# A decoder layer on one core: the opening of the kernel written out in source order

## The chip, the core and the metric

The kernel runs on one core of a Trainium2 chip. A core has five engines that run at the same time and wait for one another through semaphores: PE (TensorE, the matrix engine; its weight loads are listed as PEld), DVE (VectorE), ACT (ScalarE), POOL (GpSimd) and SP (SyncE, which here only issues DMA transfers). Each engine works through its own list of instructions in order; an instruction that waits holds up all behind it on that engine. Data lie in main memory (HBM), in the core's working memory (SBUF, 128 partitions) and in the matrix engine's result memory (PSUM, eight banks, written by PE).

The metric is the device time of one execution in microseconds (us); smaller is better. A profile is one execution recorded instruction by instruction. Its *span* runs from the first to the last instruction; the execution's own time is a little longer. The profile also records the clock that PE was granted: 1.00 is full speed.

## The reference, cut to what matters

A batch of 16 sequences of 256 tokens with 512 features goes through one decoder layer: causal self-attention, a long convolution against a context, and a feed-forward step, each followed by a residual sum and a layer norm. All projections use weights rounded to three values (-1, 0, 1) with one scale per weight matrix, and activations rounded to 8 bits with one scale per token.

```python
def _bitlinear(x, w):
    sw = 1.0 / clip(mean(abs(w)), 1e-05, None)          # one number per weight matrix
    wq = clip(round(w * sw), -1.0, 1.0) / sw
    sx = 127.0 / clip(max(abs(x), axis=-1), 1e-05, None)  # one number per token
    xq = clip(round(x * sx), -128.0, 127.0) / sx
    return einsum('bse,oe->bso', xq, wq)

q, k, v = _bitlinear(x, w_q), _bitlinear(x, w_k), _bitlinear(x, w_v)
attn = softmax(where(causal, q k^T / sqrt(32), -1e30))
x = layernorm(x + _bitlinear(attn v, w_o))
x = layernorm(x + long_convolution(ctx, ctx, x, ssm_kernel, D))
x = layernorm(x + feed_forward(x, gamma, W))           # W rounded to three values as well
```

So there are five weight matrices of 512 x 512 (`w_q`, `w_k`, `w_v`, `w_o`, `w_f`). Each needs, before it can be used: the mean of its absolute values (a sum along each partition, then a sum over the partitions), the reciprocal of that, a scaling and rounding (adding the large number MAGIC rounds a float to an integer), a clamp to -1..1, and a store as bf16.

## The kernel before, in words

The kernel has three parts, one after the other.

**The opening (lines 37 to 126).** All inputs of the opening are loaded: `first` (batch 0 of x, 0.5 MB) and the five raw weights (1 MB each) over the two DMA queues of SP and ACT, then the convolution's taps (`rows`, 80 KB). GpSimd builds constants (`ident`, `mask_f`, `pick_f`, `col`). Then a loop over the five weights (L99 to L121) does for each: the absolute sum (L104 on DVE for the first three, L107 on ACT for the last two), the sum over partitions as a product with a matrix of ones (`total`, L109), the scale and its inverses (L111 to L116), the two rounding passes (L119 and L120, on DVE for weights 0 and 2, on POOL for weights 1, 3 and 4), and the bf16 store on ACT (L121). `rows` gets its diagonal term and is written to main memory as `taps` (L124, L125). The order of these instructions on each engine is not the source's: this part stands outside the block whose order is written by hand, and a planner has placed it.

**Layer 1, the attention (lines 160 to 481).** It works on one batch at a time, in a software pipeline: `step(b)` holds, in four groups g = 0..3, stages of several batches. For batch b + 1 it does `scan` (the scores once, only for the row maxima), for b `weigh` (scores again, exponential) and `values`, for b + 2 `turn_in`, `project_qk` and `project_v` (the three projections), for b + 3 `fetch_x` and the rounding of x (`fetch_scales`, `fetch_scaled`, `fetch_rounded`), for b - 1 the output projection, and for b - 2 the norm and `keep`, which stores the result, transposed, in `x1t`. `x1t` is one large SBUF tile that layer 2 reads. `step(-2)`, with the first batch's projections, is still placed by the planner; from `step(-1)` on the order on PE, ACT, DVE and POOL is the source's (`tc.manual_schedule`, L479). The DMA queues of SP are not in that list.

Scores of `scan` and `weigh` share one four-bank PSUM tile `s`: `scan` of one group cannot start before the reader of the previous scores is done. The small results (`acc`, `tp`, `row`, `total` in the changed kernel) rotate through three banks under the tag `misc`.

**Layer 2, convolution and feed-forward (lines 484 to 714).** It loops over 32 heads. For each head SP loads `c` (two transfers, L512 and L513) and `w` (L516, from `taps`); POOL multiplies pairs (`kv`, L521), PE does the convolution as matrix products (`y`, L546), and so on. Its SBUF tiles take the addresses that layer 1's pools gave back, and wait for the last users of those addresses. Which tiles meet which addresses follows from the order in which the pools are opened: layer 1's pool `xp` (x as loaded: `xt`, `xr`) is opened inside layer 1 and given back with it.

## Time and profile before

| what | value |
|---|---|
| median of 3 runs | 982.52 us (981.02 to 983.88) |
| the profiled execution's own time | 980.88 us |
| its span | 979.0 us |
| mean granted PE clock | 0.978 |
| busy share of the span | PE 89%, DVE 75%, POOL 50%, ACT 42% |
| weights landed (w_q, w_k, w_v, w_o, w_f) | 9.9, 13.1, 15.3, 18.5, 21.2 us |
| first product with a rounded weight (`acc`, L220) | 39.42 us |
| first scores (`scan`, L259) | 46.16 us |
| first product of layer 2 (`y`, L546) | 515.01 us |

A line of the timeline reads: start, duration, engine, line, operation, result <- operands, shapes, count; in brackets how long the engine was idle before it and what ended that. A line of windows reads: the stretch, then for each engine the busy time and the number of instructions, the granted clock, the DMA engines' busy share and the rate in GB/s. PE is busy nearly all the time, except in the first 46 us, around 60 us, around the border of the two layers near 500 us, and at the very end.

### The profile page before, as it was taken

The numbers are of one execution on the slowest core, as the hardware profiler recorded it, in microseconds if no ns is written. First come the engines' busy times: TensorE is split into PE (matmuls) and PEld (weight loads), VectorE is DVE, ScalarE is ACT, GpSimd is POOL, SyncE is SP. The second block draws the span as 40 slices with busy tenths as digits, with TensorE's granted clock in tenths as the row PEclk, the third lists the DMA queues.
The fourth block names the chain that finished last, engine by engine and source line by source line (L and its number), as shares of the span: only waits on it lengthen the run. The fifth ranks groups of instructions, "written<-read, shape, count | busy, mean of one in ns | idle before, by whom it ended". The sixth has DMA issues, their size and how long they took to land.

```text
span 979.0 us, 21212 instructions
## 1 busy us (share of the span) xinstructions
PE 867.2 (89%) x8349; PEld 626.0 (64%) x8426; DVE 734.5 (75%) x1947; ACT 415.7 (42%) x651; POOL 488.4 (50%) x569
## 2 busy tenths in 40 slices
PE   1488999999999999998758999999999999999992
PEld 1255666666666666665526777777777777777771
DVE  6465777777777777776444898888988898889885
ACT  2624565665656666665541232223322332223222
POOL 4413233222323323222228778777787778777850
PEclk9999999999999999999978999999999999999996
DMA  9000110011111110000022222122212222222100
GB/s 322 28 22 24 45 44 24 24 44 45 45 45 45 45 45 2 24 23 23 24 68 67 65 76 65 50 76 76 71 43 76 76 73 54 64 76 75 33 12 33
DMA packets 54739, 53.18 MB, mean 54 GB/s; under 512 B 19120, under 2 KB 35504, under 8 KB 54640
## 3 DMA queue, kind: packets, MB, share of 16 engines
q1 hardware_dynamic: 52816, 48.33, 16.7%
q10 hardware_dynamic: 1824, 3.49, 1.0%
q8 instruction: 67, 1.10, 0.4%
q14 instruction: 32, 0.26, 0.1%
HBM read 43.34 MB, written 8.47 MB: 53 GB/s over the span
## 4 chain that ended last, share of the span: by engine, by line
PE 53%; DVE 31%; ACT 6%; issue 6%; DMA 2%; POOL 2%; SPq 0%; ACTq 0%; DVEq 0%; POOLq 0%
PE y L546 8%; PE acc L220 6%; PE s L292 6%; PE pv L324 5%; PE s L259 4%; DVE st L582 4%; PE sums L331 4%; DVE turn L567 3%; PE acc_o L387 3%; PE acc_f L641 3%; PE tp L148 3%; PE acc_v L232 3%; DVE full L601 2%; PE s L252 2%; DVE r L643 2%
## 5 line engine op out<-in xcount | busy, mean ns | idle before, releaser
L546 PE MATMUL y<-kv,w 128*128 128x288 f32 x1280 | 335.2, 409 | 4.4 <-DMA c<-in_ctx_t 2.9
L546 PEld LDWEIGHTS y<-kv,w 128*128 128x128 f32 x1280 | 235.3, 192 | 60.5 <-POOL kv L521 5.6
L308 POOL TENSOR_SCALAR_AFFINE_SELECT p<-p 128x512 f32<-128x512 f32 x128 | 78.5, 638 | 256.9 <-ACT p L304 256.9
L673 POOL TENSOR_TENSOR own<-own,turn 128x512 f32<-128x512 f32 x128 | 162.9, 1273 | 78.6 <-DVE turn L567 60.7
L521 POOL TENSOR_TENSOR kv<-c 128x512 f32<-128x512 f32 (+1 forms) x192 | 182.2, 965 | 34.7 <-PE y L546 29.7
L264 DVE TENSOR_REDUCE nmax<-s 128x4 f32<-128x512 f32 (+1 forms) x128 | 116.6, 954 | 42.6 <-PE s L259 41.3
L304 ACT ACTIVATE p<-s 128x1536 f32<-128x1536 f32 x64 | 93.1, 1454 | 88.1 <-PE s L299 88.1
L590 ACT ACTIVATE root<-quarter 128x2 f32<-128x2 f32 x64 | 13.0, 203 | 210.2 <-DVE quarter L588 210.2
L575 PE MATMUL tok<-ident,own 128*128 128x128 f32 x640 | 91.0, 273 | 0.0
L575 PEld LDWEIGHTS tok<-ident,own 128*128 128x128 f32 x640 | 75.5, 141 | 16.2
L554 DVE SCALAR_TENSOR_TENSOR own<-y,q 128x128 f32<-128x128 f32 x128 | 36.0, 281 | 53.0 <-PE y L546 52.9
L220 PE MATMUL acc<-xit,w 128*128 128x256 bf16 x512 | 67.9, 278 | 5.8 <-ACT xit L149 5.8
L557 DVE TENSOR_TENSOR own<-y,q 128x384 f32<-128x384 f32 x128 | 69.7, 544 | 0.0
L567 DVE TENSOR_TENSOR turn<-y,q 128x384 f32<-128x384 f32 x128 | 69.6, 543 | 0.0
L292 PE MATMUL s<-qt,kt 32*128 32x256 f32 (+1 forms) x1024 | 60.4, 350 | 2.6 <-DVE nmax L264 2.5
L220 PEld LDWEIGHTS <-w 128*128 128x128 bf16 x512 | 46.2, 99 | 23.3 <-issue 13.4
L259 PE MATMUL s<-kt,qt 32*128 32x128 f32 (+1 forms) x1024 | 60.7, 352 | 0.0
L324 PE MATMUL pv<-p,va 128*32 128x256 f32 (+1 forms) x1024 | 55.9, 334 | 4.7 <-POOL p L308 3.3
L292 PEld LDWEIGHTS s<-qt,kt 32*128 32x128 f32 x1024 | 47.0, 186 | 17.1 <-issue 14.6
L331 PE MATMUL sums<-p,col 128*32 128x256 f32 (+1 forms) x1024 | 54.4, 329 | 0.0
L224 DVE SCALAR_TENSOR_TENSOR qt<-acc,q_scale,inv_row 128x512 f32<-128x512 f32 x32 | 24.0, 750 | 39.5 <-PE acc L220 39.4
L388 DVE SCALAR_TENSOR_TENSOR r<-acc_o,o_mul,xr 128x512 f32<-128x512 f32 x32 | 24.0, 750 | 38.0 <-PE acc_o L387 36.3
(125 smaller groups left out, 1355.5 us busy)
## 6 DMA issues: line engine op xcount, KB each, us to landing
xr<-in_x SPq DMA_DIRECT2D x16, 512.0 KB, 3.4
c<-in_ctx_t SPq DMA_DIRECT2D x32, 256.0 KB, 3.3
w<-taps SPq DMA_DIRECT2D x32, 256.0 KB, 3.6
out_y<-res SPq DMA_DIRECT2D x32, 256.0 KB, 2.3
xt<-in_x SPq DMA_DIRECT2D x15, 512.0 KB, 3.5
c<-in_ctx_t SPq DMA_DIRECT2D x32, 128.0 KB, 3.2
raw<-in_w_q ACTq DMA_DIRECT2D x1, 1024.0 KB, 9.1
raw<-in_w_k SPq DMA_DIRECT2D x1, 1024.0 KB, 11.8
```

Source lines behind the costliest of these rows:

```text
L220: nc.tensor.matmul(acc[:, j, :], w[:, c, o * P : (o + 1) * P], m.xit[:, c].rearrange("p t k -> p (t k)"), start=(c == 0), stop=(c == NB - 1),)
L259: nc.tensor.matmul(s[:, r, lo:hi], m.qt[rows, g, q0 : q0 + P], m.kt[rows, g, 0:nk], start=False, stop=True, skip_group_check=True,)
L264: nc.vector.tensor_reduce(view(m.nmax, t * NH + g, [[NB, 4]]), s[:, :, cols], AX.X, ALU.max, negate=True)
L292: nc.tensor.matmul(s[:, r, lo:hi], m.kt[rows, g, k0 : k0 + P], m.qt[rows, g, q0:S], start=(lo == 0), stop=False, skip_group_check=True,)
L304: nc.scalar.activation(p, s[:, :, 0 : 3 * P], AF.Exp)
L324: nc.tensor.matmul(acc[rows, q0:S], m.va[:, j, 4 * g + r, :], p[:, r, src], start=(j == 0), stop=(j == 1), skip_group_check=True, tile_pos ...
L331: nc.tensor.matmul(m.sums[rows, q0:S], col[:, g, :], p[:, r, src], start=(g == 0 and j == 0), stop=(g == NB - 1 and j == 1), skip_group_ch ...
L521: nc.gpsimd.tensor_tensor(kv[:, :, at : at + n * B].rearrange("p c (i b) -> p c i b", b=B), c[:, :, i : i + n, :], c[:, :, i + d : i + d + ...
L546: nc.tensor.matmul(y[:, Y0 + k * HALF : Y0 + (k + 1) * HALF], lhs, kv[:, mb, k * HALF : (k + 1) * HALF], start=(mb == 0), stop=(mb == lb),)
L567: nc.vector.tensor_tensor(view(t, B, [[P + B, 3], [1, P]]), view(y, Y0 + AT + P, [[P, 3], [1, P]]), view(q, base, [[0, 3], [1, P]]), ALU.mult,
L575: nc.tensor.matmul(tok[:, lb, :], lhsT=own[:, d, :], rhs=ident, is_transpose=True, start=(d == 4), stop=(d == 0))
L673: nc.gpsimd.tensor_tensor(own[:, 0:4, :], own[:, 0:4, :], turns[lb], ALU.add)
```

## The change

The change rewrites the opening and leaves layer 2 as it is.

- **Order.** The opening becomes a function `begin()` inside the block whose order is the source's. `step(-2)` is gone; `begin()` has the projections of batch 0 to queries and keys, and the rounding of batch 1. The planner orders none of it any more, except the constants and loads ahead of it.
- **Weights 0 and 1** (`w_q`, `w_k`): absolute sum on DVE and on ACT, both rounding passes on DVE, in two halves of 1024 columns, each half stored by ACT on its own.
- **Weight 2** (`w_v`): absolute sum on ACT in `begin()`; its scale and both rounding passes, on POOL, in `step(-1)` group 0; the store in group 1; the projection to values of batch 0 in group 2.
- **Weights 3 and 4** (`w_o`, `w_f`): absolute sum on ACT, passes on POOL, store on ACT, spread over `step(-1)`, `step(0)` and `step(1)`.
- **Memory.** The raw weights, `rows`, `dsk` and `mask_f` lie in parts of `x1t` (`lent`), which is not written before `step(2)`. The pool `xp` is opened ahead of layer 1 and stays open to the kernel's end, so layer 2's tiles get other addresses. Batch 0 of x uses `xp` too, and batch 1 is loaded right behind `w_k`; `w_f` moves from ACT's queue to SP's.
- **Small things.** `v_mul` is computed by a stage of its own (`values_scale`); `mask` and `pick` are copied inside `begin()`; `taps` is written at the end of `step(-1)`.

```diff
+    kept = ctx.enter_context(tc.tile_pool(name="kept", bufs=1))
+    x1t = kept.tile([P, XH, NB, XD, B], F32, name="x1t")
+    flat = x1t.rearrange("p h c i b -> p (h c i b)")
+    xp = ctx.enter_context(tc.tile_pool(name="xp", bufs=2))
+    def lent(place, n, parts=P):
+        return flat[0:parts, place * W : place * W + n]
...
+    raw = [lent(i, W) for i in range(5)]
     for i, w in enumerate((w_q, w_k, w_v, w_o, w_f)):
-        (nc.scalar, nc.sync)[i % 2].dma_start(raw[i], w.rearrange("(c p) o -> p c o", p=P))
+        (nc.scalar, nc.sync, nc.scalar, nc.sync, nc.sync)[i].dma_start(
+            raw[i].rearrange("p (c o) -> p c o", o=E), w.rearrange("(c p) o -> p c o", p=P)
+        )
+        if i == 1:
+            second = xp.tile([P, S // P, E], F32, name="xt")
+            nc.sync.dma_start(second, x[1].rearrange("(t p) e -> p t e", p=P))
...
-    for i in range(5):
-        ...
+    def weight_size(i, engine):
+        if engine is nc.vector:
+            nc.vector.tensor_reduce(parts[:, i : i + 1], raw[i], AX.X, ALU.add, apply_absolute_value=True)
+        else:
+            nc.scalar.activation(lent(5, W), raw[i], AF.Abs, accum_out=parts[:, i : i + 1])
+    def weight_scale(ps, i):
+        total = ps.tile([P, 1], F32, name="total", tag="misc")
+        nc.tensor.matmul(total, ones, parts[:, c], start=True, stop=True)
+        nc.vector.tensor_scalar(w_mul[:, c], total, 1.0 / (E * E), 1e-5, ALU.mult, ...)
+        nc.vector.reciprocal(w_mul[:, c], w_mul[:, c])
+    def weight_round(i, engine, part, n=2):   # n=1: both passes on one half; n=2: one pass on all
+        ...
+    def weight_store(i, half=None):
+        nc.scalar.activation(weights[i]...[:, c], raw[i][:, c], AF.Copy, bias=-MAGIC)
...
     with ExitStack() as l1:
-        xp = l1.enter_context(tc.tile_pool(name="xp", bufs=2))
...
 # step(b), at the ends of its groups' lists (g == 2: ahead of project_v(b + 2, 1))
+  g == 0:  if b == -1: begin_values(0)
+           elif b == 1: begin_late(4, 3)
+  g == 1:  if b == -1: begin_values(1); begin_late(3, 0)
+           elif b == 0: begin_late(3, 3); begin_late(4, 0)
+  g == 2:  on(values_scale, b + 3)
+           if b == -1: begin_values(2); begin_late(3, 1)
+           elif b == 0: begin_late(4, 1)
+  g == 3:  if b == -1: begin_late(3, 2); write_taps()
+           elif b == 0: begin_late(4, 2)
...
-        on(fetch_x, 0, 0)
-        on(fetch_scales, 0)
-        on(fetch_scaled, 0)
-        on(fetch_rounded, 0)
-        step(-2)
+        def begin():
+            m, n = batches[0:2]
+            fetch_x(m, 0)
+            fetch_x(n, 1)
+            fetch_scales(m)
+            fetch_scaled(m)
+            nc.vector.tensor_copy(mask, mask_f)
+            fetch_rounded(m)
+            weight_size(0, nc.vector)
+            turn_in(m)
+            weight_size(1, nc.scalar)
+            weight_scale(ps, 0)
+            for half in range(2):
+                weight_round(0, nc.vector, half, 1)
+                weight_store(0, half)
+            weight_scale(ps, 1)
+            for half in range(2):
+                weight_round(1, nc.vector, half, 1)
+                weight_store(1, half)
+            weight_inverse(0)
+            weight_inverse(1)
+            weight_size(2, nc.scalar)
+            fetch_scales(n)
+            fetch_scaled(n)
+            fetch_rounded(n)
+            for i in (0, 1, 2, 3):
+                project_qk(m, i)
+            nc.vector.tensor_copy(pick, view(pick_f, 0, [[1, NB], [0, P]]))
+        def begin_values(part):
+            part 0: weight_scale(ps, 2); weight_inverse(2); weight_round(2, nc.gpsimd, 0); weight_round(2, nc.gpsimd, 1)
+            part 1: weight_store(2); values_scale(batches[0]); values_scale(batches[1])
+            part 2: project_v(batches[0], 0); project_v(batches[0], 1)
+        def begin_late(i, part):
+            part 0: weight_size(i, nc.scalar); weight_scale(ps, i); weight_inverse(i)
+            part 1: weight_round(i, nc.gpsimd, 0)
+            part 2: weight_round(i, nc.gpsimd, 1)
+            part 3: weight_store(i)
         with tc.manual_schedule(engines=by_hand):
+            begin()
             for b in range(-1, B + 2):
                 step(b)
```

(The parts of `begin_values` and `begin_late` and the places in `step` are shown shortened to one line each; the calls and their order are the kernel's.)

More of the change, by code (lines that the diff above doesn't have):

```diff
@@ L38, in decoder_kernel @@
     taps_pool = ctx.enter_context(tc.tile_pool(name="taps_d", bufs=1, space=bass.MemoryType.DRAM))
-    first = const.tile([P, S // P, E], F32, name="first")
     weights = [const.tile([P, NB, E], BF16, name=f"w{i}") for i in range(5)]
@@ L43, in decoder_kernel @@
     taps = taps_pool.tile([XH, E + P], F32, name="taps")
-    wl_scope = ExitStack()
-    wl = wl_scope.enter_context(tc.tile_pool(name="wload", bufs=1))
-    wp = wl_scope.enter_context(tc.tile_pool(name="wpsum", bufs=1, space=PSUM))
+    kept = ctx.enter_context(tc.tile_pool(name="kept", bufs=1))
+    x1t = kept.tile([P, XH, NB, XD, B], F32, name="x1t")
+    flat = x1t.rearrange("p h c i b -> p (h c i b)")
+    W = NB * E
+    xp = ctx.enter_context(tc.tile_pool(name="xp", bufs=2))
+    def lent(place, n, parts=P):
+        return flat[0:parts, place * W : place * W + n]
+    first = xp.tile([P, S // P, E], F32, name="xt")
     nc.sync.dma_start(first, x[0].rearrange("(t p) e -> p t e", p=P))
-    raw = [wl.tile([P, NB, E], F32, name=f"raw{i}") for i in range(5)]
+    raw = [lent(i, W) for i in range(5)]
     for i, w in enumerate((w_q, w_k, w_v, w_o, w_f)):
-        (nc.scalar, nc.sync)[i % 2].dma_start(raw[i], w.rearrange("(c p) o -> p c o", p=P))
-    rows = wl.tile([XH, E + P], F32, name="rows")
+        (nc.scalar, nc.sync, nc.scalar, nc.sync, nc.sync)[i].dma_start(
[4 more added lines that the diff above has]
+            nc.sync.dma_start(second, x[1].rearrange("(t p) e -> p t e", p=P))
+    rows = lent(6, E + P, XH)
     nc.scalar.dma_start(rows, ker)
-    dsk = wl.tile([XH, 1], F32, name="dsk")
+    dsk = lent(7, 1, XH)
     nc.scalar.dma_start(dsk, d_skip.rearrange("(h o) -> h o", o=1))
@@ L65, in decoder_kernel @@
     nc.gpsimd.memset(half, -0.5)
-    mask_f = wl.tile([P, 2, P], F32, name="mask_f")
+    mask_f = lent(7, 3 * P)[:, P : 3 * P].rearrange("p (j k) -> p j k", j=2)
     nc.gpsimd.memset(mask_f, 0.0)
@@ L75, in decoder_kernel @@
     mask = const.tile([P, 2, P], BF16, name="mask")
-    nc.vector.tensor_copy(mask, mask_f)
-    pick_f = wl.tile([P, NB], F32, name="pick_f")
+    pick_f = const.tile([P, NB], F32, name="pick_f")
     nc.gpsimd.memset(pick_f, 0.0)
@@ L87, in decoder_kernel @@
     pick = const.tile([P, NB, P], BF16, name="pick")
-    nc.vector.tensor_copy(pick, view(pick_f, 0, [[1, NB], [0, P]]))
     col = const.tile([P, NB, DH], F32, name="col")
@@ L96, in pow_neg_half @@
         nc.gpsimd.tensor_tensor(dst, src, half[:, : src.shape[1]], ALU.pow)
-    for i in range(5):
-        t = raw[i].rearrange("p c o -> p (c o)")
-        early = i < 3
-        part = wl.tile([P, 1], F32, name=f"part{i}")
-        if early:
-            nc.vector.tensor_reduce(part, t, AX.X, ALU.add, apply_absolute_value=True)
-        else:
-            size = wl.tile([P, NB * E], BF16, name="size")
-            nc.scalar.activation(size, t, AF.Abs, accum_out=part)
-        total = wp.tile([P, 1], F32, name=f"total{i}", tag=f"total{i % 2}")
-        nc.tensor.matmul(total, ones, part, start=True, stop=True)
-        mean = wl.tile([P, 1], F32, name=f"mean{i}")
-        nc.vector.tensor_scalar(mean, total, 1.0 / (E * E), 1e-5, ALU.mult, ALU.max if i < 4 else ALU.add)
-        w_mul = wl.tile([P, 1], F32, name=f"w_mul{i}")
-        nc.vector.reciprocal(w_mul, mean)
-        nc.vector.reciprocal(w_inv[:, i : i + 1], w_mul)
+    wq, wk, wv, wo, wf = weights
@@ new lines, in decoder_kernel @@
+    parts = const.tile([P, 5], F32, name="parts")
+    w_mul = const.tile([P, 5], F32, name="w_mul")
+    def weight_size(i, engine):
+        if engine is nc.vector:
+            nc.vector.tensor_reduce(parts[:, i : i + 1], raw[i], AX.X, ALU.add, apply_absolute_value=True)
+        else:
+            nc.scalar.activation(lent(5, W), raw[i], AF.Abs, accum_out=parts[:, i : i + 1])
+    def weight_scale(ps, i):
+        total = ps.tile([P, 1], F32, name="total", tag="misc")
+        c = slice(i, i + 1)
+        nc.tensor.matmul(total, ones, parts[:, c], start=True, stop=True)
+        nc.vector.tensor_scalar(w_mul[:, c], total, 1.0 / (E * E), 1e-5, ALU.mult, ALU.max if i < 4 else ALU.add)
+        nc.vector.reciprocal(w_mul[:, c], w_mul[:, c])
@@ L115, in decoder_kernel, with weight_inverse @@
+    def weight_inverse(i):
+        nc.vector.reciprocal(w_inv[:, i : i + 1], w_mul[:, i : i + 1])
         if i == 0:
             nc.vector.tensor_scalar(q_scale, w_inv[:, 0:1], 1.0 / math.sqrt(DH), None, ALU.mult)
-        engine = nc.vector if i in (0, 2) else nc.gpsimd
-        engine.tensor_scalar(t, t, w_mul, MAGIC, ALU.mult, ALU.add)
-        engine.tensor_scalar(t, t, MAGIC + 1.0, MAGIC - 1.0, ALU.min, ALU.max)
-        nc.scalar.activation(weights[i].rearrange("p c o -> p (c o)"), t, AF.Copy, bias=-MAGIC)
@@ L122, in decoder_kernel @@
-    wq, wk, wv, wo, wf = weights
-    nc.vector.tensor_tensor(rows[:, P - 1 : P], rows[:, P - 1 : P], dsk, ALU.add)
-    nc.sync.dma_start(taps, rows)
-    wl_scope.close()
-    kept = ctx.enter_context(tc.tile_pool(name="kept", bufs=1))
-    x1t = kept.tile([P, XH, NB, XD, B], F32, name="x1t")
+    def weight_round(i, engine, part, n=2):
+        both = (
+            lambda t: engine.tensor_scalar(t, t, w_mul[:, i : i + 1], MAGIC, ALU.mult, ALU.add),
+            lambda t: engine.tensor_scalar(t, t, MAGIC + 1.0, MAGIC - 1.0, ALU.min, ALU.max),
+        )
+        if n == 1:
+            t = raw[i][:, part * W // 2 : (part + 1) * W // 2]
+            both[0](t)
+            both[1](t)
+        else:
+            both[part](raw[i])
@@ L132, in scaled, with write_taps @@
+    def weight_store(i, half=None):
+        c = slice(0, W) if half is None else slice(half * W // 2, (half + 1) * W // 2)
+        nc.scalar.activation(weights[i].rearrange("p c o -> p (c o)")[:, c], raw[i][:, c], AF.Copy, bias=-MAGIC)
+    def write_taps():
+        nc.vector.tensor_tensor(rows[:, P - 1 : P], rows[:, P - 1 : P], dsk, ALU.add)
+        nc.sync.dma_start(taps, rows)
     def scaled(pool, tag, src, mul, engine=nc.vector):
@@ L177, in fetch_x @@
         def fetch_x(m, b):
-            if b == 0:
-                m.x = first
+            if b < 2:
+                m.x = (first, second)[b]
             else:
@@ L187, in fetch_scales, with values_scale @@
             m.mul, m.inv = absmax_scales(sp, "x", amax, NT)
+        def values_scale(m):
             m.v_mul = sp.tile([P, NT], F32, name="v_mul")
@@ L446, in step @@
                     on(divide, b - 1, 1)
+                    if b == -1:
+                        begin_values(0)
+                    elif b == 1:
+                        begin_late(4, 3)
                 elif g == 1:
@@ L452, in step @@
                     on(project_qk, b + 2, 2)
+                    if b == -1:
+                        begin_values(1)
+                        begin_late(3, 0)
+                    elif b == 0:
+                        begin_late(3, 3)
+                        begin_late(4, 0)
                     on(keep, b - 2, b - 2)
@@ L460, in step @@
                     on(fetch_scales, b + 3)
+                    on(values_scale, b + 3)
+                    if b == -1:
+                        begin_values(2)
+                        begin_late(3, 1)
+                    elif b == 0:
+                        begin_late(4, 1)
                     on(project_v, b + 2, 1)
@@ L471, in step @@
                     on(fetch_rounded, b + 3)
-        by_hand = {mybir.EngineType.PE, mybir.EngineType.Activation, mybir.EngineType.DVE, mybir.EngineType.Pool}
-        on(fetch_x, 0, 0)
-        on(fetch_scales, 0)
-        on(fetch_scaled, 0)
-        on(fetch_rounded, 0)
-        step(-2)
+                    if b == -1:
+                        begin_late(3, 2)
+                        write_taps()
+                    elif b == 0:
+                        begin_late(4, 2)
+        by_hand = {mybir.EngineType.PE, mybir.EngineType.Activation, mybir.EngineType.DVE, mybir.EngineType.Pool}
@@ new lines, in begin_values @@
+        def begin_values(part):
+            if part == 0:
+                weight_scale(ps, 2)
+                weight_inverse(2)
+                weight_round(2, nc.gpsimd, 0)
+                weight_round(2, nc.gpsimd, 1)
+            elif part == 1:
+                weight_store(2)
+                for b in range(2):
+                    values_scale(batches[b])
+            else:
+                for t in range(NT):
+                    project_v(batches[0], t)
+        def begin_late(i, part):
+            if part == 0:
+                weight_size(i, nc.scalar)
+                weight_scale(ps, i)
+                weight_inverse(i)
+            elif part == 1:
+                weight_round(i, nc.gpsimd, 0)
+            elif part == 2:
+                weight_round(i, nc.gpsimd, 1)
+            else:
+                weight_store(i)
```

## The prediction

> **What bounds the kernel now.** I read the page first: its slices show PE at nine tenths nearly throughout and low only in the first two slices and near the border of the layers. So the change can win only before 46 us, and can lose wherever it puts a new wait ahead of PE. Next the timeline of the opening (start, duration, engine, line), because it says what each weight costs on each engine:

> ```profile
> PE   1488999999999999998758999999999999999992
> ...
> 19.25 2.80 DVE L119 TENSOR_SCALAR raw<-raw,w_mul 128x2048 f32<-128x2048 f32 x1
> 25.06 1.26 DVE L119 TENSOR_SCALAR raw<-raw,w_mul 128x2048 f32<-128x2048 f32 x1
> 29.58 1.90 POOL L120 TENSOR_SCALAR raw<-raw 128x2048 f32<-128x2048 f32 x1
> 29.63 1.87 DVE L189 TENSOR_SCALAR v_mul<-x_v,w_inv 128x2 f32<-128x2 f32 x1
> 31.51 1.91 ACT L121 ACTIVATE w<-raw 128x2048 bf16<-128x2048 f32 x1 [1.09 <-POOL raw L120]
> 39.42 4.21 PE L220 MATMUL acc<-xit,w 128*128 128x256 bf16 x24 [4.82 <-ACT xit L149]
> 46.16 0.94 PE L259 MATMUL s<-kt,qt 32*128 32x128 f32 x16
> ```

> The same DVE pass takes 1.26 alone and 2.80 beside a POOL pass, and a DVE pass over two columns takes 1.87 because it ends where the POOL pass ends (31.5): the two exclude each other. PE gets its first weight product at 39.42, after all five weights are done, and the first scores at 46.16.

> Then the windows around the idle stretch at 60 us (stretch, busy PE, PEld, DVE, ACT, POOL, then granted clock): 3.24 us without PE work are followed by 3.41 us at half clock.

> ```profile
> 58.94:62.18 3.24, 0.00 (x0) 0.00 (x1) 3.05 (x8) 0.00 (x0) 2.52 (x4) 1.00 0.11 16
> 62.18:62.86 0.68, 0.68 (x10) 0.45 (x10) 0.00 (x0) 0.36 (x2) 0.00 (x0) 1.00 0.86 322
> 62.86:66.27 3.41, 3.41 (x27) 2.36 (x26) 1.70 (x2) 1.59 (x5) 0.00 (x0) 0.50 0.19 74
> ```

> Last the timeline where the change puts new work: step(0), and the border of the layers, where SP's load of `c` follows the last reader of `xr` (506.64) and POOL's first product the last transposes (512.14).

> ```profile
> 74.13 1.45 ACT L304 ACTIVATE p<-s 128x1536 f32<-128x1536 f32 x1 [1.28 <-PE s L299]
> 75.63 0.60 PE L252 MATMUL s<-mask,ident_h 128*128 128x256 bf16 x4 [0.56 <-ACT p L304]
> 82.09 1.22 POOL L308 TENSOR_SCALAR_AFFINE_SELECT p<-p 128x512 f32<-128x512 f32 x2 [5.22 <-ACT p L304]
> 83.46 0.17 DVE L154 TENSOR_SCALAR x_v<-amax 128x2 f32<-128x2 f32 x1
> ...
> 505.89 0.75 DVE L388 SCALAR_TENSOR_TENSOR r<-acc_o,o_mul,xr 128x512 f32<-128x512 f32 x1 [0.95 <-PE acc_o L387]
> 506.70 0.64 SPq L512 DMA_DIRECT2D c<-in_ctx_t  x1
> 510.17 1.97 PE L419 MATMUL tp<-ident,r 128*128 128x128 f32 x8 [4.32 <-ACT r L410]
> 512.27 8.18 POOL L521 TENSOR_TENSOR kv<-c 128x512 f32<-128x512 f32 x9 [3.26 <-DMA w<-taps]
> ```

> **The change part by part.** I follow the changed kernel's own order and waits with durations of this profiled execution.

> *1. Up to the first scores.* x lands at 6.9 and POOL's `diag` ends at 11.63 as before. PE then does `row` (1.20) and two groups of transposes (0.61 each), 14.1; the first `total` (0.56) and two small DVE ops give 15.1. Four half passes on DVE: 0.44 for 512 columns (the pass on `oq_t`) and 1.26 for 2048 give 0.70 for 1024, so 2.8, with POOL idle: 17.9. ACT meanwhile sums |w_k| (14.7 to 16.8). Scale 0.35 and four half passes: 21.05. ACT's last half store, between 0.61 (512 columns) and 1.91 (2048), is 1.05: 22.1. PE then has 22 products left, at the 24 in 4.21 of the row above 3.9: 26.0; mask 0.6, first scores at 26.6 against 46.16: **-19.5** (-20.5 if the clock comes at once, -18.0 if it comes a window later or half passes cost 0.85). The loads do not set this: w_k landed at 13.1, and the queues ahead of it are the same. `w_f`, now on SP's queue, waits there for w_q's landing (9.9), and behind it wait x of batch 2 and `xr`; they are needed 20 us later.

> *2. step(-1), groups 0 and 1.* The same 3.0 us as before (46.16 to 49.16) lead to the next `acc`, 29.6 to 30.65. PE's `total` for w_v follows (0.3), DVE gives its scale at 31.9. Then the chain has no cover: two POOL passes (1.90 each) to 35.8, ACT's store 1.91 to 37.75, ACT's |w_o| 1.91 and its readout 0.2 to 39.9. PE's `total` for w_o waits for that, and behind it on PE waits the mask of scan group 2, ready at 34.3. It starts at 40.2 where the old one started at 53.45: the gain is down to 13.25, so this part costs **+6.25** (6.0 to 8.4, the upper end with POOL passes of 2.94, seen when DVE held it up).

> [...] The rows here say 1.90 against 1.26, 1.5 times for a one-input pass. [...]

> *3. step(-1), group 2* has batch 0's two value projections, 0.86 each: **+1.7** (they stood ahead of the first scores before; no cover, PE is full there).

> *4. The clock.* PE idles 5.6 us before that `total`. The idle of 3.24 above was followed by a half-clock window in which 16 `s` took 1.67 instead of 0.94, `row` 1.22 instead of 0.70, eight `tp` 1.01 instead of 0.61: 1.65 lost. **+1.65** (0 to 3.3, for no window or two). The old idle near 60 us stays: scan group 3, `lay` and its transposes keep their order, and `lay`'s casts did not stretch beside POOL's `diag` (0.20 at 61.70), so POOL's new pass there costs nothing, 1.4 if it did.

> *5. step(0), group 1.* Before, the mask of scan group 2 followed the exponential's end within 0.05 us (75.58, 75.63). Now ACT stores w_o (1.91) and sums |w_f| (1.91 + 0.1) first, and PE's `total` for w_f waits for the sum with the mask behind it: **+4.3** (4.1 to 4.6). PE idles 4.5 us: **+1.65** (0 to 3.3) for the clock again.

> *6. step(0), group 2.* POOL's first pass on w_f starts when the selects end (83.31), and DVE's `x_v` at 83.46 and `v_mul` behind it are passes of the kind that sat 1.87. nmax is queued behind them and scores of weigh group 3 wait for it with 0.1 us to spare: 85.25 instead of 83.46, **+1.8** (0 to 2.1).

> *7. Other late pieces.* POOL's second pass on w_f lies between selects that end at 89.8 and begin at 95.4; ACT's store of w_f falls into ACT's idle 4.1 us before 99.4; `taps` is read 400 us later, and its DMA on SP waits for a 0.14 us DVE op at the end of step(-1) with only x of a batch three steps ahead behind it. On DVE, the casts of `ident_h` and `mask` (0.22, 0.29) fit between 8.56 and w_q's landing at 9.9, `pick` (0.42) and the inverses (0.15) run while PE works, and the two `v_mul` (0.20) lie in the stall of part 2. Nothing, 1.9 for each weight pass if its cover failed.

> *8. The border of the layers.* With `xp` kept open, `c` takes the addresses of tiles that PE's last transposes free together with the rest, so its load is issued after 512.14, not at 506.70. The first one landed 3.4 after its issue in this trace (median 3.3, 3.0 to 5.8 over all), and POOL's first product, which began at 512.27, starts at 515.7. PE's `y` waits for POOL's products, and `w`, third in the queue (landed 6.1 after the first issue), arrives at 518.3, just as the third product ends. **+3.4** (3.0 to 5.5; no gain is possible, since the load now waits for what the product waited for).

> Sum: -19.5 + 6.25 + 1.7 + 1.65 + 4.3 + 1.65 + 1.8 + 3.4 = **+1.25**. Span 980.3, with the 1.9 around it 982.1. The profiled execution (980.88) stood 1.6 under the median of the runs, so the forecast as a median is 982.52 + 1.25 = **983.8**.

> [...]

> **The rivals.**

> *Slower.* The half clock lasts two windows after each of the two new stalls. For it: the half-clock window began 0.68 after the work at 62.18 did, so it is not tied to the end of an idle stretch, and a stretch may touch two. Against: after 62.18 it was one window. Price 2 x 1.65: +4.55, 987.1. It decides from one extra window on (+2.9).

> *Faster.* The grid falls so that neither new stall nor the old idle is followed by a half-clock window: -3 x 1.65, in all -3.7, 978.8. For it: the idle of 3.24 lay almost wholly in one window, a worse split could have gone unseen. Against: 5.6 and 4.5 us can hardly avoid filling most of one.

> *The gain survives at the border.* Were the load of `c` as early as before, 3.4 less: -2.15, 980.4, within the bound still. Against: the new addresses.

> *No exclusion for two-column passes* (part 6 free): -0.55, 982.0. Against: the 1.87.

> **How the numbers follow.** 0.3%, 2.95 us, is about what a measurement of this kernel can tell from no change (the three runs span 2.9). Likeliest: all parts about as summed, or with one of the two small rivals, between 979.6 and 985.4: 0.52. Slower rival, or a part at its upper end (POOL 2.94, the landing 5.5): 0.35. Faster: 0.13. The range for 8 in 10 reaches to 979.0 and, to take in the slower rival, 987.8; the likeliest's own is 980.4 to 985.4. Faster 0.13, same 0.52, slower 0.35.

> **What would show it.** First scores near 26.6; PE idle from 34.3 to about 39.9, ended by ACT's |w_o|; the mask of group 2 in step(0) more than 4 us after the exponential; a two-column DVE pass of some 1.8 beside L135 on POOL there; half clock after both stalls; SP's first `c` just after the last transposes and POOL waiting over 3 us for it. The prediction is wrong if an exclusion or a weight pass costs other than its row, if POOL and ACT overlap more than their order allows, or if the border hides the load.

## The result, and the profile after

The changed kernel takes 988.28 us (median of 4 executions, 987.43 to 989.11) against 981.77 us before: a ratio of 1.0063 with a 95% interval of 1.0051 to 1.0075. A second measurement gave 987.44 us (6 executions) against 982.70, 1.0048 (1.0035 to 1.0062). So the change makes the kernel slower, by about half a per cent. The profiled execution took 987.43 us with a span of 985.7, 6.7 more than before, where the prediction had said +1.25. In medians it had said 983.8, with 979.0 to 987.8 as its range for 8 in 10.

The page of the changed kernel, its busy tenths and the granted clock in 40 slices:

```profile
PE   3768999999999999998757999999999999999992
...
PEclk9878999999999999999977999999999999999996
```

PE is as busy as before in most slices, but the second to fourth slice (24.6 to 98.6 us) now run at seven to eight tenths of the clock. The timeline of the changed kernel gives the marks that the prediction named: first scores, the two `total` products, the blocked two-column pass, the border. With them stands a cast of `lay`, the laying out of the row maxima (L296), that met POOL's second pass on `w_o`.

```profile
26.13 0.94 PE L282 MATMUL s<-kt,qt 32*128 32x128 f32 x16
39.29 0.59 PE L123 MATMUL total<-parts,ones 128*128 128x1 f32 x2 [5.83 <-ACT x1t L118]
40.68 1.67 PE L282 MATMUL s<-kt,qt 32*128 32x128 f32 x16
50.57 1.89 POOL L136 TENSOR_SCALAR x1t<-x1t 128x2048 f32<-128x2048 f32 x1
51.37 1.13 DVE L296 CAST terms<-nmax 128x32 bf16<-128x32 f32 x1
71.18 0.58 PE L123 MATMUL total<-parts,ones 128*128 128x1 f32 x2 [4.25 <-ACT x1t L118]
81.22 1.98 POOL L135 TENSOR_SCALAR x1t<-x1t,w_mul 128x2048 f32<-128x2048 f32 x1
81.39 1.83 DVE L176 TENSOR_SCALAR x_v<-amax 128x2 f32<-128x2 f32 x1
85.42 1.12 PE L315 MATMUL s<-qt,kt 32*128 32x256 f32 x16 [2.37 <-DVE nmax L287]
...
513.33 1.97 PE L442 MATMUL tp<-ident,r 128*128 128x128 f32 x8 [4.32 <-ACT r L433]
515.39 0.64 SPq L608 DMA_DIRECT2D c<-in_ctx_t  x1
518.96 8.16 POOL L617 TENSOR_TENSOR kv<-c 128x512 f32<-128x512 f32 x9 [6.78 <-DMA c<-in_ctx_t]
```

Every wait that the sum priced is where the prediction put it. What it did not have is mostly in the windows (stretch, then busy time of PE, PEld, DVE, ACT and POOL, the granted clock, DMA share and GB/s), here cut where the clock changes:

```profile
34.83:38.25 3.42, 0.00 (x0) 0.00 (x0) 0.72 (x2) 2.81 (x2) 0.57 (x1) 1.00 0.00 0
38.25:41.66 3.41, 2.37 (x18) 1.80 (x22) 0.49 (x3) 0.99 (x2) 1.23 (x1) 0.50 0.01 2
41.66:45.07 3.41, 3.19 (x17) 1.38 (x11) 1.82 (x2) 0.69 (x1) 0.74 (x1) 0.50 0.00 0
45.07:48.49 3.42, 3.42 (x20) 1.75 (x18) 2.34 (x5) 1.69 (x3) 0.53 (x1) 1.00 0.00 0
48.49:51.90 3.41, 0.95 (x17) 0.54 (x16) 2.36 (x3) 0.37 (x1) 3.33 (x5) 1.00 0.40 133
51.90:55.31 3.41, 2.08 (x18) 1.55 (x22) 1.22 (x5) 1.42 (x3) 0.56 (x1) 0.50 0.16 47
55.31:58.73 3.42, 3.39 (x26) 2.09 (x26) 1.82 (x2) 1.42 (x3) 0.00 (x0) 0.50 0.00 0
...
82.62:86.03 3.41, 1.04 (x24) 0.78 (x20) 3.27 (x8) 0.21 (x1) 3.03 (x5) 1.00 0.01 2
86.03:89.45 3.42, 2.13 (x30) 1.13 (x22) 0.30 (x2) 2.48 (x4) 1.03 (x3) 0.50 0.46 154
89.45:92.86 3.41, 3.41 (x27) 2.35 (x26) 1.71 (x2) 0.82 (x3) 2.16 (x2) 0.50 0.00 0
```

There are four half-clock stretches between 38 and 93 us (38.25, 51.90, 68.97 and 86.03), each two windows of the clock or 6.83 us long; before there was one window of 3.41. Below, a half window is such a window of 3.41 us at half clock. Marks of the two traces, in us from the start of the span, show where the 20 us were given back:

| mark | before | after | difference | change of it | forecast |
|---|---|---|---|---|---|
| first scores | 46.16 | 26.13 | -20.03 | -20.0 | -19.5 |
| mask of scan group 2, step(-1) | 53.45 | 39.74 | -13.71 | +6.3 | +6.25 |
| mask of scan group 3, step(-1) | 57.47 | 47.97 | -9.50 | +4.2 | +1.7 and clock 1.65 |
| transposes `tpn` | 62.18 | 53.23 | -8.95 | +0.55 | 0 |
| exponential, step(0) group 0 | 67.68 | 59.53 | -8.15 | +0.8 | 0 |
| mask of scan group 2, step(0) | 75.63 | 71.63 | -4.00 | +4.15 | +4.3 |
| exponential, step(0) group 2 | 80.58 | 78.50 | -2.08 | +1.9 | clock 1.65 |
| `nmax`, step(0) group 3 | 83.86 | 83.46 | -0.40 | +1.7 | +1.8 |
| exponential, step(1) group 0 | 93.83 | 95.61 | +1.78 | +2.2 | 0 |
| last transposes of layer 1 | 510.17 | 513.33 | +3.16 | +1.4 | 0 |
| first product `kv` of layer 2 | 512.27 | 518.96 | +6.69 | +3.5 | +3.4 |

### The profile page after: what moved, and what is told of

Read it like the earlier page. It is cut to its first block, busy times and chain, and to the rows that moved or that the text cites. A ratio compares the mean times of both kernels' runs of the same rounds, so it can differ in the third digit from the quotient of the medians.

```text
span 985.7 us, 21212 instructions
## 1 busy us (share of the span) xinstructions
PE 875.7 (89%) x8350; PEld 629.3 (64%) x8426; DVE 729.5 (74%) x1949; ACT 420.1 (43%) x657; POOL 486.7 (49%) x569
## 4 chain that ended last, share of the span: by engine, by line
PE 54%; DVE 31%; ACT 7%; issue 6%; POOL 1%; DMA 1%; ACTq 0%; DVEq 0%; POOLq 0%; SPq 0%
PE y L642 8%; PE acc L243 6%; PE s L315 6%; PE pv L347 5%; PE s L282 5%; DVE st L678 4%; PE sums L354 4%; PE acc_v L255 3%; PE tp L170 3%; DVE turn L663 3%; PE acc_o L410 3%; PE acc_f L737 3%; PE s L275 3%; DVE full L697 2%; DVE r L739 2%
## 5 line engine op out<-in xcount | busy, mean ns | idle before, releaser
L327 ACT ACTIVATE p<-s 128x1536 f32<-128x1536 f32 x64 | 92.9, 1452 | 89.8 <-PE s L322 89.8
L282 PE MATMUL s<-kt,qt 32*128 32x128 f32 (+1 forms) x1024 | 63.6, 365 | 0.0
L745 ACT ACTIVATE res<-r,shift,res 128x512 f32<-128x512 f32 x32 | 26.0, 813 | 58.6 <-issue 50.0
```

The source lines that it names most:

```text
L282: nc.tensor.matmul(s[:, r, lo:hi], m.qt[rows, g, q0 : q0 + P], m.kt[rows, g, 0:nk], start=False, stop=True, skip_group_check=True,)
L327: nc.scalar.activation(p, s[:, :, 0 : 3 * P], AF.Exp)
```

## The experiments

Two theories stood. *Clock:* the waits cost what the sum said, and the rest is PE's half clock, which lasts two windows after each idle stretch. *Waits:* the loss lies in the waits, and the half clock falls where PE has slack. Differences below are medians against 987.9, the middle of the changed kernel's two measurements (988.28 and 987.44); ratios are to the kernel before, run beside each. Executions of one kernel spread over 1.3 to 4.1 us.

**The border undone, and the border alone.** The first kernel is the changed one with `xp` given back when layer 1 ends, the second the one before with only `xp` kept open.

```diff
 # changed kernel, border undone
-    xp = ctx.enter_context(tc.tile_pool(name="xp", bufs=2))
+    l1 = ExitStack()
+    xp = l1.enter_context(tc.tile_pool(name="xp", bufs=2))
...
-    with ExitStack() as l1:
+    with l1:
 # kernel before, border alone
-        xp = l1.enter_context(tc.tile_pool(name="xp", bufs=2))
+        xp = ctx.enter_context(tc.tile_pool(name="xp", bufs=2))
```

> The changed kernel with one thing undone: the pool xp is opened where the change opens it, but given back with layer 1. Both theories agree on the sum's part 8 (the border): the load of c is issued about 5 us before the last transposes end, POOL's first product no longer waits over 3 us for it, and the time falls by 3.4 to 3.6 us against the changed kernel's 988.3, to about 984.8. The rival, that the border only inherits a lateness from elsewhere, expects 988.3.

> The kernel before with only this part of the change: xp is kept open to the kernel's end. Part 8 alone expects +3.4 to +3.6 us against the kernel before, about 985.3, and the load of c issued right after the last transposes. If the address had nothing to do with it: no change.

Measured: 984.26 us (-3.6; ratio 1.0020, 1.0012 to 1.0029) and 985.94 us (+4.0 against 981.92; ratio 1.0039, 1.0025 to 1.0053). The timelines, first with the border undone, then the border alone:

```profile
509.65 0.65 SPq L609 DMA_DIRECT2D c<-in_ctx_t  x1
513.12 1.97 PE L443 MATMUL tp<-ident,r 128*128 128x128 f32 x8 [4.32 <-ACT r L434]
515.22 8.16 POOL L618 TENSOR_TENSOR kv<-c 128x512 f32<-128x512 f32 x9 [3.25 <-DMA w<-taps]
```

```profile
512.26 1.97 PE L419 MATMUL tp<-ident,r 128*128 128x128 f32 x8 [4.32 <-ACT r L410]
514.32 0.64 SPq L512 DMA_DIRECT2D c<-in_ctx_t  x1
517.48 8.15 POOL L521 TENSOR_TENSOR kv<-c 128x512 f32<-128x512 f32 x9 [6.37 <-DMA c<-in_ctx_t]
```

From the start of the last transposes to POOL's first product it takes 2.1 us when the load of `c` was issued before them, and 5.2 us (5.6 in the changed kernel) when it was issued after. The border is a cost of its own, at the size that part 8 gave it.

**PE kept busy while it waits.** Four blocks of extra products into PSUM that nobody reads; every other instruction stays, and the waits keep their length within about 0.2 us.

```diff
+        def keep_busy(pool, n):
+            out = pool.tile([P, E], F32, name="idle", tag="sums" if pool is ps_o else "misc")
+            for _ in range(n):
+                nc.tensor.matmul(out, ident_h, wq[:, 0, :], start=True, stop=True)
 # step(-1), g == 1, ahead of begin_late(3, 0):   keep_busy(ps_o, 24)
 # step(-1), g == 3, after lay:                   keep_busy(ps_o, 15)
 # step(0), g == 1, ahead of begin_late(4, 0):    keep_busy(ps, 17)
 # step(0), g == 3, after values(0, 2):           keep_busy(ps, 10)
```

> The changed kernel with 66 extra products of 128 x 512 into memory that nobody reads, put on PE at the four places of the opening where it idles over 2 us (24 ahead of total for w_o, 15 ahead of the transposes of step(-1), 17 ahead of total for w_f, 10 ahead of the second scores of group 3 in step(0)). They leave every wait as long as it is and take only the idleness from PE. Clock theory (what the prediction missed is half clock that follows idle stretches of PE, two windows each): no half clock between 38 and 93 us, and 988.3 - 0.86 - 0.8 - 0.3 - 1.9 - 2.2 of what was missed, with the two windows priced in the sum (3.3) gone as well, so about 979 to 981. Waits theory (the loss lies in the waits themselves and the half clock falls where PE has slack): 988 or a little more.

Measured: 978.39 us (-9.5; ratio 0.9965, 0.9952 to 0.9978). With 66 products more than the changed kernel it is faster than both. Its timeline and windows where the first wait lies:

```profile
33.92 5.34 PE L455 MATMUL idle<-w,ident_h 128*128 128x512 bf16 x24
39.91 0.38 PE L123 MATMUL total<-parts,ones 128*128 128x1 f32 x2 [0.64 <-ACT x1t L118]
```

```profile
35.46:38.88 3.42, 3.42 (x17) 1.54 (x16) 0.71 (x2) 2.83 (x2) 0.56 (x1) 1.00 0.00 0
38.88:42.29 3.41, 2.77 (x28) 1.47 (x27) 1.09 (x5) 0.97 (x2) 1.45 (x1) 1.00 0.01 2
42.29:45.70 3.41, 3.41 (x22) 1.91 (x21) 3.34 (x7) 1.85 (x3) 0.52 (x1) 1.00 0.00 0
```

`total` still waits for ACT's sum and starts at 39.91 (39.29 without the extra products), but the clock stays at 1.00, here and until 479 us. The wait did not change and the loss went: the waits theory falls. Of the 9.5 us, the marks put about 8.1 at the four places and 1.4 at a half-clock stretch near 465 us that this execution did not have: from the exponential of step(1) to the last transposes it took 416.3 us, the changed kernel 417.7.

**One place at a time.** The same blocks, first the last one alone, then the first alone.

> The changed kernel with 10 of the extra products, at the last of the four places alone (PE's idle 2.4 us before the second scores of group 3 in step(0)); x_v still waits out POOL's pass. Clock theory: no half clock from 86.0 to 92.9 us, -2.2 us against the changed kernel, about 986.1; together with the run that moved POOL's pass (-3.2) it parts that run's gain into a wait of 1.0 to 1.7 and a clock of 1.5 to 2.2. Waits theory: 988.3.

> The changed kernel with 24 of the extra products, at the first place alone (PE's idle 5.8 us before total for w_o). The sum priced the half clock there at 1.65 for one window. Clock theory with two windows: from the mask of scan group 2 to that of group 3 takes 5.7 instead of 8.2 us and the time falls by 2.5, to 985.8. One window: 1.65 less, 986.6. Waits theory: 988.3.

Measured: 984.80 us (-3.1; ratio 1.0024, 1.0014 to 1.0034) and 985.07 us (-2.8; ratio 1.0032, 1.0020 to 1.0044). With the last block there is no half clock from 76.7 to 486 us, so none near 465 us either, which the changed kernel had for 3.41 us; that second part was not foreseen and, at 1.4 us in the marks, may be why it won 3.1 and not 2.2. At the place itself, from the mask of scan group 3 in step(0) to that of group 1 in step(1), it is 15.57 us instead of 17.75. With the first block the mask of group 3 follows that of group 2 after 5.73 us instead of 8.23 (39.74 to 47.97):

```profile
39.66 0.60 PE L275 MATMUL s<-mask,ident_h 128*128 128x256 bf16 x4
45.39 0.60 PE L275 MATMUL s<-mask,ident_h 128*128 128x256 bf16 x4
```

So the half clock after that stall is worth 2.5, not the 1.65 of the sum.

**The wait behind the last place.** POOL's first pass on `w_f` is moved next to its second.

```diff
 # step(b)
-                    elif b == 0:          # g == 2
-                        begin_late(4, 1)
...
                     elif b == 0:          # g == 3, at the end
+                        begin_late(4, 1)
                         begin_late(4, 2)
```

> The changed kernel with POOL's first pass on w_f moved from step(0) group 2 to the end of group 3, next to the second. Part 6 alone (the two-column pass x_v waits out POOL's pass): x_v takes 0.17 instead of 1.83 and the time falls by 1.7, to 986.6. With the clock theory PE's idle stretch before the second scores of group 3 shrinks from 2.4 to 0.7 us, the half clock of 86.0 to 92.9 goes too, and the time falls by 3.9, to 984.4.

Measured: 985.12 us (-2.8; ratio 1.0027, 1.0018 to 1.0036), between the two values, so the trace has to tell:

```profile
80.42 0.17 DVE L176 TENSOR_SCALAR x_v<-amax 128x2 f32<-128x2 f32 x1
80.82 1.81 DVE L287 TENSOR_REDUCE nmax<-s 128x4 f32<-128x512 f32 x2
```

`x_v` takes 0.17 instead of 1.83. From the mask of scan group 3 in step(0) to that of group 1 in step(1) it is 13.90 us (79.17 to 93.07) instead of 17.75 (80.14 to 97.89), 3.85 less: the wait and the clock behind it, as the clock theory had it. The profiled execution took 982.69 us, the second least of twelve (982.52 to 985.76). Why the median won only 2.8 goes with the clock: three executions with a mean granted clock of 0.968, this one among them, took 982.5 to 983.4 us, three with 0.966 took 984.2 to 984.9, and six with 0.963 or 0.964 took 985.4 to 985.8. So the longer ones had more half clock; where it lay in them is not recorded.

**The sums earlier.** ACT sums `w_o` and `w_f` in step(-1) group 0, where it idled 6.35 us, and PE has both `total` products right behind `project_qk`.

```diff
 # step(b), g == 0, after turn_in
+                    if b == -1:
+                        weight_size(3, nc.scalar)
+                        weight_size(4, nc.scalar)
 # g == 1, b == -1
-                        begin_values(1)
                         begin_late(3, 0)
+                        begin_late(4, 0)
+                        begin_values(1)
 # g == 1, b == 0
-                        begin_late(4, 0)
 # begin_late, part 0
-                weight_size(i, nc.scalar)
```

> The changed kernel with the absolute sums of w_o and w_f moved to ACT's idle time in step(-1) group 0, and both total products to group 1 right behind project_qk: nothing on PE waits for ACT's store and sum any more. By the sum's own parts: 6.25 of part 2 shrinks to the store of w_v that project_v waits for, about 1; part 5 (4.3) goes; the clock of both stalls (two windows each by the clock theory, 2.5 and 1.9) goes. About -12, 976. Waits theory, without the clock: about -9, 979.

Measured: 975.17 us (-12.7; ratio 0.9927, 0.9913 to 0.9941). The mask of group 2 in step(-1) comes at 35.42 instead of 39.74, and the one in step(0) is 6.45 us after that of group 1 instead of 10.60.

**Everything together.** Border undone, early sums, POOL's pass moved, and the four value projections of step(-1) put behind scan group 3, where PE waits for `lay`.

> All that the runs point to in one kernel: xp given back with layer 1 (-3.5), the early sums (-12), POOL's first pass on w_f at the end of step(0) group 3 (-3.9), and the four value projections of step(-1) behind scan group 3, where PE idles 3.8 us for the laying out of the maxima (-3.4, and its half clock -2.4). Added up 988.3 - 25 = about 963. If the idle before the transposes of step(-1) stays, or POOL's pass on w_o meets the laying out: 966 to 968. Waits theory: about 970.

Measured: 964.91 us (-23.0; ratio 0.9830, 0.9812 to 0.9848), 2 us behind the sum. The profiled execution is the longest of the four (967.88 us at a mean clock of 0.975, the others 963.75 to 965.68 at 0.978), so some half clock is in it that the others lack. But its timeline shows a cost of the kernel's own: two-column and other small passes of DVE now met both of POOL's passes on `w_o`.

```profile
36.16 1.98 POOL L136 TENSOR_SCALAR x1t<-x1t,w_mul 128x2048 f32<-128x2048 f32 x1
36.31 1.97 DVE L213 TENSOR_SCALAR v_mul<-x_v,w_inv 128x2 f32<-128x2 f32 x2
40.05 1.03 PE L276 MATMUL s<-mask,ident_h 128*128 128x256 bf16 x4 [2.43 <-DVE nmax L288]
44.88 1.93 POOL L137 TENSOR_SCALAR x1t<-x1t 128x2048 f32<-128x2048 f32 x1
45.10 1.76 DVE L299 CAST terms<-rest 128x32 bf16<-128x32 f32 x1
```

So in a last version these two passes follow the selects of step(0) group 0, beside passes of DVE that read PSUM.

```diff
 # g == 0
+                    elif b == 0:
+                        begin_late(3, 1)
+                        begin_late(3, 2)
 # g == 2 and g == 3, b == -1
-                        begin_late(3, 1)
-                        begin_late(3, 2)
```

> The kernel with everything together, with both of POOL's passes on w_o moved from step(-1) (where v_mul sat 1.97 and a cast of lay 1.76 beside them) to the end of step(0) group 0, where POOL is idle 5.2 us and DVE only reads PSUM. By the exclusion of two-column passes v_mul gets 1.6 to 1.8 and the cast 1.6 shorter; the mask of scan group 3 follows that of group 2 by about 3.2 instead of 4.9 us. Clock theory: PE's idle there falls from 2.4 to under 1 us, no half clock before step(0), another 1.5 to 2. Together 3.5 to 5 less than 964.9: 960 to 961.5. If w_o's passes in the new place hold something up instead: 963 or more.

> The changed kernel itself, unaltered, timed once more beside the others: both theories expect 988.3 within its runs' spread (987.4 to 989.1). By the grid reading of the clock theory the half clock before step(0) group 0 may last one window or two from one execution to the next, 1 us apart.

Measured: 961.32 us (-26.6; ratio to the kernel before 0.9787, 0.9773 to 0.9801) and 987.44 us for the unaltered changed kernel. The timeline of this last version:

```profile
36.19 0.34 DVE L213 TENSOR_SCALAR v_mul<-x_v,w_inv 128x2 f32<-128x2 f32 x2
38.48 0.61 PE L276 MATMUL s<-mask,ident_h 128*128 128x256 bf16 x4 [0.97 <-DVE nmax L288]
42.49 0.25 DVE L297 CAST terms<-nmax 128x32 bf16<-128x32 f32 x1
```

`v_mul` takes 0.34 for both batches, the mask of group 3 follows that of group 2 (35.07) by 3.4 us, and from the rise of the clock at 25.8 us there is no half clock until 466 us. At 2.1% less than before, this version keeps the gain of the new opening. The repeated profile of the changed kernel had three half windows in its first stretch (36.20 to 46.44), again two in that before step(0), not one: how many there are changes from one execution to the next.

## Why the prediction was wrong

- **Part 1** (-19.5): -20.0. Right.
- **Part 2** (+6.25): +6.3, the chain of POOL, ACT and PE as written. Right, and the early sums show that it could be avoided.
- **Part 3** (+1.7): with the clock of part 4 it made +4.2, and the run with the first block shows 2.5 of that to be clock, which leaves the 1.7.
- **Part 4, the clock after the stall: this is the step that failed.** It took one window of 1.65 after each new stall, and nothing anywhere else. After the first stall two windows followed, and the run with the first block shows 2.5. The old idle near 60 us, which "stays", stays as idle time; but it too got a second window: from the transposes `tpn` to the exponential it took 6.30 us, 5.50 before, so +0.8. With the border undone, where one window followed, it took 5.35.
- **Part 4, `lay`'s casts** (0, 1.4 as a bound): +0.55. The first cast took 1.13 beside POOL's second pass on `w_o`. The row used for the zero, a pass beside POOL's `diag`, was no stand-in for a pass beside 2048 columns.
- **Part 5** (+4.3, clock 1.65): +4.15 and +1.9. The wait was right, the clock a little small.
- **Part 6** (+1.8): +1.7. Right, but the sum stopped there. It priced the wait on DVE and not what PE's idle 2.37 us would do to the clock: +2.2 in the marks, shown by the run that fills only this idle time (-2.18 there).
- **Part 7** (0): nothing of it shows among the marks.
- **Part 8** (+3.4): +3.5, and two runs, -3.6 and +4.0 (the latter has an extra half window near 464 us in its profile).
- **Nobody's part:** +1.4 between 100 us and the end of layer 1, with one half window near 465 us. The kernel before with only `xp` kept open, whose opening is the old one, has that half window too (417.7 us from the exponential of step(1) to the last transposes, as in the changed kernel, against 416.3 before). So the new opening is not its cause; it is where the clock's windows happened to fall.

The clock cost 8.8 us in the marks (2.5 + 0.8 + 1.9 + 2.2 + 1.4) against 3.3 in the sum. That is the whole error of 5.5 between the profiles; between the medians it is 4.5. Only 1.1 of it comes from the two stalls whose half clock the sum priced. The other 4.4 comes from places where it put the clock at nothing: behind the old idle (0.8), behind part 6's wait (2.2) and near 465 us (1.4).

The rival *Slower* named the effect: a half-clock stretch is not tied to the end of the idle time and may be two windows, as it was four times in the changed kernel's profile. That its time, 987.1, comes near 988.3 is luck. It added 3.3 for second windows after the two new stalls, where 1.1 was measured; the rest came from places that it did not name. Its reason against itself, "after 62.18 it was one window", was a single case, and that case was the luck of the grid, as the next part but one shows.

## What to carry to other kernels

Price an idle stretch of PE twice: the wait itself, and the half clock after it, and do this also for stretches that are only 2 us long (2.37 us of idle time were followed by 6.83 us at half clock here, +2.2) and for those that were there before and are merely moved (+0.8). Filling such a stretch, with work that can be moved there or even with products for nothing, is worth the clock alone: about 8 us here for four places. Weight preparation on an engine that is slower at it (here 1.90 us for a pass on POOL, 1.26 on DVE) is not hidden because the engine is free: the waits for it cost +6.3 and +4.15 here. What it needs at its start (the sum, the scale) has to be ready early, and its passes have to lie where no small `tensor_scalar` or cast of DVE in SBUF meets them (1.83 instead of 0.17, 1.13 instead of 0.26).

## What the runs showed of the hardware

```profile
48.40:51.81 3.41, 1.81 (x23) 0.94 (x21) 1.86 (x5) 1.05 (x2) 3.00 (x5) 1.00 0.16 47
51.81:55.23 3.42, 1.24 (x22) 0.95 (x22) 2.04 (x6) 0.92 (x3) 1.41 (x1) 1.00 0.38 130
55.23:58.64 3.41, 3.40 (x26) 2.25 (x22) 1.82 (x2) 1.94 (x4) 0.00 (x0) 0.50 0.01 2
```

Here the work begins before the half-clock stretch and fills it, and one window is all. Near 465 us it is the same grid: work of 1.21 to 1.62 us in one stretch brings half clock in seven of the twelve profiles, and where the same idle time is spread over two stretches (2.11 and 2.51 us of work in the kernel before) there is none. The thresholds are what these profiles show; that the chip decides by exactly this count was not tested.

PE need not be idle for a whole stretch: 2.37 us of idle time before 85.42 sufficed, and 2.43 in the first version with everything together. Within an execution the changes of the clock lie whole multiples of 3.41 us apart, wherever the work begins: 38.25, 45.07, 51.90 and 58.73 in the changed kernel, where PE's work after the first two waits begins at 39.29 and 53.23.

**Small passes beside POOL.** A `tensor_scalar` of DVE over two columns in SBUF took 0.17 to 0.22 alone and 1.83 to 1.87 when it started with a 2048-column pass of POOL; casts of 32 columns took 0.18 to 0.26 alone and 1.13 to 1.76 beside one. They end about when POOL's pass ends: `v_mul` at 31.50 and the pass at 31.48 in the kernel before, `x_v` at 83.22 and the pass at 83.20, the cast at 52.50 and the pass at 52.46 in the changed one. Not every pass of DVE was held up: two reductions of 512 columns that read PSUM (`nmax`) took their usual 1.82 together beside it in the last version (at 51.41, POOL's pass from 51.11 to 53.09), and `amax`, a reduction that reads SBUF, took 1.20 at 27.70 in the kernel before, inside a POOL pass (26.55 to 29.49), as it does elsewhere (1.20 to 1.22).
